# Last image's z loaded with channels outermost, its outputs in the tiles of y, and a cast moved from ScalarE to GpSimd

## Chip, cores and metric

The kernel runs on one core of one Trainium2 chip. The metric is the device time of one execution in microseconds (us); lower is better. The engines are named as in the profile: PE is TensorE (PEld its weight loads), DVE is VectorE, ACT is ScalarE, POOL is GpSimd and SP is SyncE, which here only issues DMAs.

## The reference, cut to what matters

The input x is 16 images of 56 x 56 pixels and 384 channels in f32. Two layers follow each other, each with a group normalisation over 32 groups of 12 channels and a residual addition.

```python
# layer 0: dilated attention; three groups of channels with dilations 1, 2, 3; 12 heads of 32 channels
qkv = einsum('bchw,oc->bohw', groupnorm(x), w_qkv)
attn = softmax(einsum('bgdn,bgdkn->bgnk', q, unfold3x3(k, dil)) * 32 ** -0.5)
y = einsum('bgnk,bgdkn->bgnd', attn, unfold3x3(v, dil))
x = x + einsum('bhwc,oc->bhwo', y, w_proj) + b_proj
# layer 1: depthwise 3x3 convolution with weights binarised to their sign
x = x + depthwise3x3(groupnorm(x), sign(w))
```

## The kernel before

An image is cut into 7 chunks of 8 rows, that is 448 pixels; there are 112 chunks. A chunk passes three plans. `plan_a` loads x, turns it so that channels lie on partitions and writes it to a scratch tensor `xd` in DRAM, taking statistics. `plan_b` is the attention: project q, k and v, score the nine neighbours, softmax, weigh v, project the output, add the residual and write the result to a scratch tensor `x1d` in DRAM, taking statistics again. `plan_c` is the convolution: it loads `x1d` back, normalises it, applies the taps, adds the residual, turns the result back to pixels on partitions and writes the output.

Each piece of work of a plan is registered with `at(when, order, piece)`: a step number, with 9 steps per chunk, and a class that orders the pieces within a step. The classes are listed once, SOFTMAX first, then SCORE, STATISTICS, CONVOLVE, WEIGH, QUERY, SPREAD, QKV, PROJECT and so on, LOADS last. The pieces are then emitted in sorted order. A tile framework turns them into one instruction queue per engine, in which instructions run strictly in order, and inserts the waits; it may move instructions of one queue against each other when it builds the program. DMAs from SP and ACT share eight completion semaphores in turn.

The softmax of a chunk ends in the f32 tile `ew`. TensorE spreads the weights over channels in bf16, so `ew` is split into three bf16 terms in the tile `e3`: `softmax_3` casts `ew` to the first term on ACT (L558) and subtracts it on POOL, giving `rest` (L559); `softmax_4` casts `rest` to the second term on ACT (L563) and subtracts that on POOL, giving the third term (L564). `turn_weights` sends `e3` through a DMA transpose into `aT` (L569). `weigh` then multiplies: TensorE spreads into `pb_a` (L582), DVE multiplies with v into a tile `w` (L589, three such buffers), POOL adds up the products (L597, L600, L601) into the tiles `y` (pool `y_p`, four buffers of 128 x 448), and `out_project` uses them (`po`, L615).

In `plan_c`, two of the three blocks of 128 channels (j = 0, 1) are convolved on TensorE. A tile `z` holds 32 channels (one of four sets q) on three times 32 partitions, one third for each row shift ky, so that one matmul sums over the three rows. The third block goes through nine multiply-adds: on ACT and POOL for images 0 to 14 (L768, L774), on DVE for the last image (`taps_last`, L759), whose loads and work nothing else overlaps any more. For the last image `z` lives in buffers that the attention has left: four of pool `t_p` for even chunks; three of `w_p` and the one of `xr_p` for odd chunks; each holds two sets q. So the loads of chunk c+2 wait until chunk c has been convolved. `normalise` scales them in place (L703 on ACT, L699 on DVE for q = 3), `convolve` runs 24 matmul instructions for each j (`pc`, L717) and DVE adds the residual (L724). `turn` transposes the result (`pt_o`, L789), copies it out of PSUM on ACT to `osb` (L791; pool `o_p`, two buffers) and stores it (L794), on SP for images 0 to 14, on ACT for the last.

The loads of `z` have two forms. Images 0 to 14, and the first and last chunk of the last image, use one DMA per row shift ky (L684), with 32 channels outermost. The five middle chunks of the last image use one DMA per set q (L692), which reads the three shifted rows as the outermost dimension of its source:

```python
one = by_set[:, q, p0 - W : p0 - W + PX]
three_rows = bass.AP(one.tensor, one.offset, [(W, 3), *one.ap])
nc.sync.dma_start(set_of(j, q), three_rows)
```

The functions that the diff touches, and what calls them:

Of the kernel before, what the change touches and what calls it, by code (L numbers as in the profile page):

```python
# [8 lines left out]
F32 = mybir.dt.float32  # L9
# [8 lines left out]
P = 128  # L18
# [4 lines left out]
NQ = 4  # L23
ROWS = 8
SUB = 112
# [10 lines left out]
def dilated_attention_then_binary_conv(  # L36
# [28 lines left out]
    nc = tc.nc  # L65
    B, H, W, C = x.shape
    PX = ROWS * W
    NCH = H // ROWS
# [82 lines left out]
    y_p = ctx.enter_context(tc.tile_pool(name="y_p", bufs=4))  # L151
# [5 lines left out]
    o_p = ctx.enter_context(tc.tile_pool(name="o_p", bufs=2))  # L157
# [234 lines left out]
    def at(when, order, piece):  # L392

        pieces.setdefault((when, order), []).append(piece)
# [50 lines left out]
    def plan_b(m, t0):  # L445

        b, c = divmod(m, NCH)
# [104 lines left out]
        e8 = ew.rearrange(EIGHTS, k=8)  # L552
        term = [e3.rearrange("p s u (r k) -> p (s u r) k", r=4)[:, :, 8 * t : 8 * t + 8] for t in range(TERMS)]

        def softmax_3():

            had["rest"] = rest = s_p.tile([SUB, NSUB * NPAD * HEADS], F32, tag="rest", name="rest")
            nc.scalar.copy(term[0], e8)  # L558
            nc.gpsimd.tensor_tensor(rest.rearrange(EIGHTS, k=8), e8, term[0], ALU.subtract)  # L559

        def softmax_4():
            r8 = had["rest"].rearrange(EIGHTS, k=8)
            nc.scalar.copy(term[1], r8)  # L563
            nc.gpsimd.tensor_tensor(term[2], r8, term[1], ALU.subtract)  # L564

        def turn_weights():
# [67 lines left out]
        at(t0 + 9, SOFTMAX, softmax_1)  # L634
        at(t0 + 10, SOFTMAX, softmax_2)
        at(t0 + 11, SOFTMAX, softmax_3)
        at(t0 + 12, SOFTMAX, softmax_4)
        at(t0 + 12, LOADS, turn_weights)
        for i in range(9):
            at(t0 + 14 + i, WEIGH, lambda i=i: weigh(i))  # L640
# [4 lines left out]
    def plan_c(m, t0):  # L645

        b, c = divmod(m, NCH)
        p0 = c * PX
        had = {}

        def edges(j):
            found = []
            for z, _, _ in had[f"z{j}"]:
                if c == 0:
                    found.append(z[0:HD, :, 0:W])
                if c == NCH - 1:
                    found.append(z[2 * HD : 3 * HD, :, PX - W : PX])
            return found

        def set_of(j, q):  # L660
            return next(z[:, q - q0] for z, q0, q1 in had[f"z{j}"] if q0 <= q < q1)

        def load(j):
            by_set = x1d[b].rearrange("(j q c) n -> j c q n", q=NQ, c=HD)[j]
            if b < B - 1:
                z = z_p.tile([P, NQ * PX], F32, tag="z", name="z")[:K3].rearrange("p (q n) -> p q n", q=NQ)
                had[f"z{j}"] = [(z, 0, NQ)]
            else:

                had[f"z{j}"] = []  # L670
                for q0 in range(0, NQ, 2):
                    pool, tag = (t_p, "t") if c % 2 == 0 else (w_p, "w") if (j, q0) != (1, 2) else (xr_p, "xr")
                    z = pool.tile([P, 3, PX], F32, tag=tag, name="z_last")[:K3, :2]
                    had[f"z{j}"].append((z, q0, q0 + 2))
            for edge in edges(j):
                nc.gpsimd.memset(edge, 0.0)
            for ky in range(3):
                lo = W if c == 0 and ky == 0 else 0
                hi = PX - W if c == NCH - 1 and ky == 2 else PX
                n0 = p0 + (ky - 1) * W  # L680
                for z, q0, q1 in had[f"z{j}"]:
                    if b == B - 1 and 0 < c < NCH - 1:
                        continue
                    nc.sync.dma_start(  # L684
                        z[ky * HD : (ky + 1) * HD, :, lo:hi], by_set[:, q0:q1, n0 + lo : n0 + hi]
                    )
            if b == B - 1 and 0 < c < NCH - 1:

                for q in range(NQ):
                    one = by_set[:, q, p0 - W : p0 - W + PX]  # L690
                    three_rows = bass.AP(one.tensor, one.offset, [(W, 3), *one.ap])
                    nc.sync.dma_start(set_of(j, q), three_rows)  # L692

        def normalise(j):
            mrz = mr1[b][1]
# [88 lines left out]
        def turn(s):  # L784
            pt = ps_mt.tile([P, 512], F32, tag="mt", name="pt_o")
            mid = had["xg"][:, 1 : ROWS + 1, :].rearrange("p r w -> p (r w)")
            for j in range(NG):
                src = mid if j == JG else had["x1"][:, j]
                nc.tensor.transpose(pt[:SUB, j * P : (j + 1) * P], src[:, s * SUB : (s + 1) * SUB], ident)  # L789
            osb = o_p.tile([SUB, C], F32, tag="osb", name="osb")  # L790
            nc.scalar.copy(osb, pt[:SUB, :C])  # L791

            queue = nc.sync if b < B - 1 else nc.scalar
            queue.dma_start(of[b, p0 + s * SUB : p0 + (s + 1) * SUB, :], osb)  # L794

        if b == B - 1:

            at(t0 - 12, LOADS, load_g)
            at(t0 - 3, LOADS, load_x)
            ahead = 8 if c else 1  # L800
            at(t0 - ahead, NORM, normalise_g)
            for j in range(JG):
                at(t0 - 12 + j, LOADS, lambda j=j: load(j))
                at(t0 - ahead + j, NORM, lambda j=j: normalise(j))
                at(t0 + 1 + j, CONVOLVE, lambda j=j: convolve(j))
            for ky in range(3):
                at(t0 + 1 + ky, CONVOLVE, lambda ky=ky: taps_last(ky))
            for s in range(NSUB):
                at(t0 + 12, STAGE_C, lambda s=s: turn(s))
            return  # L810
# [9 lines left out]
        for j in range(JG):  # L820
            at(t0 - 4 + 3 * j, LOADS, lambda j=j: load(j))
            at(t0 - 1 + 3 * j + late, NORM, lambda j=j: normalise(j))
            at(t0 + 2 + 3 * j + late, CONVOLVE, lambda j=j: convolve(j))
        for s in range(NSUB):
            at(t0 + 9 + s, STAGE_C, lambda s=s: turn(s))

    SOFTMAX, SCORE, STATISTICS, CONVOLVE, WEIGH, QUERY, SPREAD, QKV, PROJECT, STAGE_A, STAGE_C, NORM, LOADS = range(13)
# [43 lines left out]
    for m in range(N):  # L871
        plan_a(m, start_a(m))
        plan_b(m, STEP * m)
        plan_c(m, STEP * (m + 10))
# [31 lines left out]
```

## Time and profile before

| what | value |
|---|---|
| time, median of 3 runs | 5360.88 us (5352.83 to 5364.77) |
| the profiled execution, its own time | 5362.08 us |
| its span in the profile | 5360.3 us |
| mean granted TensorE clock | 0.981 |
| busy share of PE, PEld, DVE, ACT, POOL | 97%, 44%, 78%, 45%, 78% |
| first convolution of the last image on PE | 5229.86 us |
| last convolution of the last image ends | 5346.75 us |

The page gives busy time, share of the span and number of instructions of each engine, then the span in 40 slices, in which a digit is a tenth. A row of a group reads: line, engine, operation, tiles and shapes, count | busy us in all, mean ns of one | idle time of the engine just before these instructions, and what ended it. In a timeline a row is start, length, engine, line, operation and count, with the idle time ahead of it in brackets. SPq and ACTq are the sequencers that issue DMAs: the length of such a row is the issue, not the transfer.

### The profile page before, as it was taken

The numbers are of one execution on the slowest core, as the hardware profiler recorded it, in microseconds if no ns is written. First come the engines' busy times: TensorE is split into PE (matmuls) and PEld (weight loads), VectorE is DVE, ScalarE is ACT, GpSimd is POOL, SyncE is SP. The second block draws the span as 40 slices with busy tenths as digits, with TensorE's granted clock in tenths as the row PEclk, the third lists the DMA queues.
The fourth block names the chain that finished last, engine by engine and source line by source line (L and its number), as shares of the span: only waits on it lengthen the run. The fifth ranks groups of instructions, "written<-read, shape, count | busy, mean of one in ns | idle before, by whom it ended". The sixth has DMA issues, their size and how long they took to land.

```text
span 5360.3 us, 76299 instructions
## 1 busy us (share of the span) xinstructions
PE 5174.7 (97%) x27333; PEld 2385.0 (44%) x27333; DVE 4189.1 (78%) x4125; ACT 2400.3 (45%) x4189; POOL 4178.0 (78%) x2839
## 2 busy tenths in 40 slices
PE   8999999999999999999999999999999999999965
PEld 4444444444444444444444444444444444444422
DVE  4887887877888788888888888887788878777754
ACT  3223444444444544444444444544444444444433
POOL 2677888878888888888888888887888888788880
PEclk8999999999999999999999999999999999999976
DMA  6444556655656555555665556655555655444443
GB/s 194 124 116 116 160 163 165 165 153 161 166 157 169 159 163 154 163 155 160 165 165 160 158 160 166 166 157 162 162 154 160 165 157 162 134 129 135 123 130 128
DMA packets 810793, 825.66 MB, mean 154 GB/s; under 512 B 359467, under 2 KB 800174, under 8 KB 810414
## 3 DMA queue, kind: packets, MB, share of 16 engines
q1 hardware_dynamic: 802430, 808.79, 54.9%
q10 hardware_dynamic: 7984, 12.00, 0.7%
q8 instruction: 216, 3.54, 0.3%
q14 instruction: 163, 1.34, 0.1%
HBM read 466.41 MB, written 231.21 MB: 130 GB/s over the span
## 4 chain that ended last, share of the span: by engine, by line
PE 77%; POOL 7%; DVE 7%; DMA 4%; ACT 2%; issue 1%; SPq 1%; POOLq 0%; ACTq 0%; DVEq 0%
PE pkv L463 23%; PE pq L463 13%; PE po L615 11%; PE ps L501 10%; PE pc L717 8%; PE pb_a L582 5%; POOL w L597 3%; DVE t L516 3%; DVE w L589 2%; PE pt_x L422 2%; PE pt_o L789 2%; POOL m L774 2%; PE pt_s L536 1%; ACT m L768 1%; DMA z_last<-x1d 1%
## 5 line engine op out<-in xcount | busy, mean ns | idle before, releaser
L597 POOL TENSOR_TENSOR w<-w 128x1344 f32<-128x1344 f32 x672 | 2051.6, 3053 | 420.6 <-DVE w L589 376.1
L589 DVE TENSOR_TENSOR w<-pb_a,v 128x1344 f32<-128x1344 f32 x1008 | 1558.9, 1547 | 266.6 <-PE pb_a L582 176.7
L516 DVE TENSOR_TENSOR t<-pq,k 128x1344 f32<-128x1344 f32 x1008 | 1536.1, 1550 | 228.9 <-PE pq L463 228.0
L463 PE MATMUL pkv<-xn,wqkvT 128*128 128x448 f32 x3924 | 1569.6, 549 | 11.7 <-ACT osb L791 5.7
L463 PEld LDWEIGHTS pkv<-xn,wqkvT 128*128 128x128 f32 x3924 | 718.4, 190 | 683.2 <-issue 637.5
L774 POOL TENSOR_TENSOR m<-m 128x1344 f32<-128x1344 f32 x210 | 644.5, 3069 | 281.7 <-ACT m L768 281.5
L615 PE MATMUL po<-y,wprojT 128*128 128x448 f32 x2016 | 834.7, 550 | 18.3 <-POOL y L601 14.7
L463 PE MATMUL pq<-xn,wqkvT 128*128 128x448 f32 x1962 | 830.7, 557 | 0.0
L703 ACT ACTIVATE z<-z,mrz 96x448 f32<-96x448 f32 x840 | 578.2, 751 | 360.9 <-DMA z<-x1d 325.3
L501 PE MATMUL ps<-t,sel 128*32 128x448 f32 x6048 | 663.4, 548 | 28.7 <-DVE t L516 28.0
L768 ACT ACTIVATE m<-zg,ktap 128x448 f32<-128x448 f32 x945 | 555.5, 658 | 274.2 <-POOL m L774 267.2
L615 PEld LDWEIGHTS po<-y,wprojT 128*128 128x128 f32 x2016 | 376.6, 192 | 375.8 <-issue 344.0
L717 PE MATMUL pc<-z,kdiag 96*32 96x440 f32 (+1 forms) x5040 | 517.6, 544 | 5.7 <-POOL z L705 4.6
L463 PEld LDWEIGHTS pq<-xn,wqkvT 128*128 128x128 f32 x1962 | 343.9, 189 | 316.9 <-issue 316.9
L601 POOL TENSOR_TENSOR y<-y,w 128x448 f32<-128x448 f32 x336 | 382.0, 1137 | 23.7
L582 PE MATMUL pb_a<-aT,spread 24*128 24x448 bf16 x3024 | 368.6, 359 | 32.5 <-DVE w L589 27.3
L600 POOL TENSOR_TENSOR y<-w 128x448 f32<-128x448 f32 x336 | 382.8, 1139 | 14.5
L618 DVE SCALAR_TENSOR_TENSOR xr<-po,bias,xr 128x448 f32<-128x448 f32 x336 | 227.5, 677 | 202.7 <-PE po L615 197.7
L724 DVE TENSOR_TENSOR x<-pc,x 128x448 f32<-128x448 f32 x224 | 139.1, 621 | 307.3 <-PE pc L717 295.0
L473 ACT COPY v<-pkv 128x448 f32<-128x448 f32 x336 | 178.6, 531 | 448.1 <-PE pkv L463 429.9
L473 ACT COPY k<-pkv 128x448 f32<-128x448 f32 x336 | 178.8, 532 | 401.5 <-PE pkv L463 401.4
L501 PEld LDWEIGHTS ps<-t,sel 128*32 128x32 f32 x6048 | 170.2, 109 | 365.7 <-issue 237.5
(131 smaller groups left out, 4324.0 us busy)
## 6 DMA issues: line engine op xcount, KB each, us to landing
z<-x1d SPq DMA_DIRECT2D x570, 224.0 KB
xr<-xd SPq DMA_DIRECT2D x112, 672.0 KB
x1d<-xr SPq DMA_DIRECT2D x112, 672.0 KB
xn<-xd SPq DMA_DIRECT2D x109, 672.0 KB
xin<-in_x_dram SPq DMA_DIRECT2D x105, 672.0 KB
xd<-xa SPq DMA_DIRECT2D x315, 224.0 KB
out_dram<-osb SPq DMA_DIRECT2D x420, 168.0 KB
x<-x1d SPq DMA_DIRECT2D x112, 448.0 KB
```

The source lines that it names most:

```text
L463: nc.tensor.matmul(dst[:, :PX], wqkvT[:, cc, o0 : o0 + P], had["xn"][:, cc, :], start=(cc == 0), stop=(cc == NG - 1))
L501: return nc.tensor.matmul(had["ps"][32 * j : 32 * j + 32, :PX], sel[:, s0 : s0 + 32], tk, start=(issued[j] == 1), stop=(issued[j] == len(r ...
L516: nc.vector.tensor_tensor(t.rearrange("p k (r w) -> p k r w", w=W), q3, k3, ALU.mult)
L582: return nc.tensor.matmul(pb[:, kx, :PX].rearrange("p (s n) -> p s n", s=NSUB), spread[rows_of, v % 2, :], had["a"][rows_of, :, v // 8, :] ...
L589: nc.vector.tensor_tensor(w.rearrange("p k (r w) -> p k r w", w=W), pb[:, :, :PX].rearrange("p k (r w) -> p k r w", w=W), three(kv[1][g][m ...
L597: nc.gpsimd.tensor_tensor(w0, w0, w, ALU.add)
L600: nc.gpsimd.tensor_tensor(y, w0[:, 0], w0[:, 1], ALU.add)
L615: nc.tensor.matmul(po[:, :PX], wprojT[:, g, j * P : (j + 1) * P], had[f"y{g}"], start=(g == 0), stop=(g == NG - 1))
L703: nc.scalar.activation(z, z, AF.Identity, bias=mrz[:, j, q, 0:1], scale=mrz[:, j, q, 1:2])
L717: return nc.tensor.matmul(pcr[q * HD : (q + 1) * HD, :, lo:hi], kdiag[:, kx, j * NQ + q, :], rows(set_of(j, q))[:, :, lo + kx - 1 : hi + k ...
L768: nc.scalar.activation(rows(t[:, kx]), zp[:, ky : ky + ROWS, kx : kx + W], AF.Copy, scale=ktap[:, o : o + 1])
L774: nc.gpsimd.tensor_tensor(had["m"], had["m"], t, ALU.add)
```

## The change

The second term of the split is cast on POOL instead of ACT, and the subtraction that gives `rest` is registered as a piece of its own with a later class in the same step. The five middle chunks of the last image load `z` in the form of all other chunks: three row shifts times two tiles for each j, 12 DMAs of 32 channels x 2 sets x 448 in place of 8 DMAs of 96 x 448 per chunk, 60 in place of 40 in all. The output tiles of the last image come from the four buffers of `y_p` instead of the two of `o_p`.

```diff
         def softmax_3():
-            had["rest"] = rest = s_p.tile([SUB, NSUB * NPAD * HEADS], F32, tag="rest", name="rest")
             nc.scalar.copy(term[0], e8)
+
+        def softmax_4():
+            had["rest"] = rest = s_p.tile([SUB, NSUB * NPAD * HEADS], F32, tag="rest", name="rest")
             nc.gpsimd.tensor_tensor(rest.rearrange(EIGHTS, k=8), e8, term[0], ALU.subtract)
 
-        def softmax_4():
+        def softmax_5():
             r8 = had["rest"].rearrange(EIGHTS, k=8)
-            nc.scalar.copy(term[1], r8)
+            nc.gpsimd.tensor_copy(term[1], r8)
             nc.gpsimd.tensor_tensor(term[2], r8, term[1], ALU.subtract)
...
         at(t0 + 11, SOFTMAX, softmax_3)
-        at(t0 + 12, SOFTMAX, softmax_4)
+        at(t0 + 11, PROJECT, softmax_4)
+        at(t0 + 12, SOFTMAX, softmax_5)
...
                 for z, q0, q1 in had[f"z{j}"]:
-                    if b == B - 1 and 0 < c < NCH - 1:
-                        continue
                     nc.sync.dma_start(
                         z[ky * HD : (ky + 1) * HD, :, lo:hi], by_set[:, q0:q1, n0 + lo : n0 + hi]
                     )
-            if b == B - 1 and 0 < c < NCH - 1:
-
-                for q in range(NQ):
-                    one = by_set[:, q, p0 - W : p0 - W + PX]
-                    three_rows = bass.AP(one.tensor, one.offset, [(W, 3), *one.ap])
-                    nc.sync.dma_start(set_of(j, q), three_rows)
...
-            osb = o_p.tile([SUB, C], F32, tag="osb", name="osb")
+            if b < B - 1:
+                osb = o_p.tile([SUB, C], F32, tag="osb", name="osb")
+            else:
+                osb = y_p.tile([P, PX], F32, tag="y", name="osb_last")[:SUB, :C]
             nc.scalar.copy(osb, pt[:SUB, :C])
```

In the program that results, the queue of GpSimd is the same but for the inserted copy, which stands right behind `rest` or, in some chunks, one instruction later.

More of the change, by code (lines that the diff above doesn't have):

```diff
@@ L555, in softmax_3 @@
         def softmax_3():
+            nc.scalar.copy(term[0], e8)
+        def softmax_4():
             had["rest"] = rest = s_p.tile([SUB, NSUB * NPAD * HEADS], F32, tag="rest", name="rest")
-            nc.scalar.copy(term[0], e8)
             nc.gpsimd.tensor_tensor(rest.rearrange(EIGHTS, k=8), e8, term[0], ALU.subtract)
-        def softmax_4():
+        def softmax_5():
             r8 = had["rest"].rearrange(EIGHTS, k=8)
-            nc.scalar.copy(term[1], r8)
+            nc.gpsimd.tensor_copy(term[1], r8)
             nc.gpsimd.tensor_tensor(term[2], r8, term[1], ALU.subtract)
```

## The prediction

> **What bounds the kernel now.** I read the first lines of the page, then the slices, then the waits of TensorE, then the end of the span in order of time.
>
> ```profile
> span 5360.3 us, 76299 instructions
> PE 5174.7 (97%) x27333; PEld 2385.0 (44%) x27333; DVE 4189.1 (78%) x4125; ACT 2400.3 (45%) x4189; POOL 4178.0 (78%) x2839
> PE   8999999999999999999999999999999999999965
> PEclk8999999999999999999999999999999999999976
> ```
>
> TensorE is busy 97%. The slices show where the missing 3% lies: the body is full, and the last two slices (134 us each) fall to 6 and 5, with the granted clock down to 7 and 6. So the span has two parts with different limits. In the body, from 500 to 5050 us, gaps of TensorE sum to only about 50 us: work moved between other engines gains almost nothing there, and costs only if it makes TensorE wait. The tail is the convolution of the last image. TensorE's timeline there gives the start of each of its seven chunks; these are the first groups of five of them:
>
> ```profile
> 5244.57 5.91 PE L717 MATMUL pc<-z_last,kdiag 96*32 96x448 f32 x48
> 5282.24 4.66 PE L717 MATMUL pc<-z_last,kdiag 96*32 96x448 f32 x24
> 5304.57 4.40 PE L717 MATMUL pc<-z_last,kdiag 96*32 96x448 f32 x24
> 5328.60 6.56 PE L717 MATMUL pc<-z_last,kdiag 96*32 96x448 f32 x48 [0.97 <-ACT osb L791]
> 5338.57 4.23 PE L717 MATMUL pc<-z_last,kdiag 96*32 96x448 f32 x24 [1.79 <-POOL z_last L705]
> ```
>
> With the starts at 5229.86 and 5259.36 the six steps between chunks are 14.7, 14.8, 22.9, 22.3, 24.0 and 10.0 us, together 108.7. The SyncE timeline of the slow steps shows what fills them:
>
> ```profile
> 5287.90 21.08 SPq L692 DMA_DIRECT2D z_last<-x1d  x9
> 5309.09 2.08 SPq L709 DMA_DIRECT2D x<-x1d  x1
> 5311.27 0.39 SPq L735 DMA_DIRECT2D xg_last<-x1d  x1
> 5328.96 7.70 SPq L684 DMA_DIRECT2D z_last<-x1d  x8
> ```
>
> SyncE is held by the loads of z in the form of L692: about 2.2 us for one. The loads of the last chunk use L684 and go out in under a us each, and the step that they feed is the short one. The windows of a slow step and of the short one (columns: length, busy us of PE, PEld, DVE, ACT, POOL, then clock, DMA share, GB/s) show the DMA engines themselves:
>
> ```profile
> 5282.20:5304.60 22.40, 12.62 (x65) 4.08 (x65) 7.98 (x13) 6.89 (x11) 0.00 (x0) 0.50 0.38 127
> 5328.60:5338.60 10.00, 8.21 (x61) 3.11 (x62) 9.36 (x16) 4.57 (x8) 0.40 (x2) 0.81 0.79 246
> ```
>
> A slow step keeps 0.38 of the 16 DMA engines busy, no compute engine is full, and yet everyone waits for data. In the 40 slices of 5260 to 5310 us the quiet ones move 75 to 77 GB/s at one to two tenths: three engines of 16 are 0.19. One L692 load is 32 channels x 3 rows x 1,792 B = 172 KB; at 76 GB/s that is 2.26 us, the time that one issue takes. Forty of them are 90 us, and they run from 5216 to 5319. **The tail is bound by three DMA engines.**
>
> **What the Trainium skill says.** "DMA: Bandwidth & Descriptors", section "Why a DMA increments its semaphore by 16 and not by 1": a DMA runs on the largest number of engines up to 16 that divides the slowest dimension of both sides. With 3 rows outermost at the source and 96 partitions at the destination that is 3; with 32 outermost on both sides it is 16. The trace agrees (75 to 77 GB/s beside two tenths). "GPSIMD Engine Reference", section "4.1 Engine selection": one-input work on GpSimd is roughly line-rate, two-input about 2x slower than VectorE. The trace has no one-input copy on GpSimd; its 112x512 memset took 514 ns, its two-input 112x512 subtraction 1,160 ns. "TensorE: Matmul & The Clock Gate", Part 1: the clock halves when TensorE is idle and recovers after about 3.4 us of sustained work. Here 24 matmuls of pc took 4.66 us in the slow steps and 2.44 us at 5234.52.
>
> **The change part by part.**
>
> *Loads of z.* The 40 L692 loads go; 60 of 32 channels x 2 sets x 448 (115 KB, the same bytes) come. The nearest row is L684's own 24 loads of z_last: issue 0.42 us in the median. Twelve per chunk are 5.0 us of SyncE, plus about 0.4 each for x and xg: 5.8. Each chunk moves 1.38 MB of z, 0.46 of x, 0.29 of xg and 0.69 of output, 2.8 MB; at the 246 GB/s of the short step 11.4 us at most, and at the 355 GB/s of the best slice 7.9. Loads of chunk c+2 wait for the convolution of c, a step and more ahead, so they leave the path. What is late next is a loop between ScalarE and TensorE. The changed program's order has, per chunk: six normalisations and one of xg, TensorE's two convolutions, its transposes of the chunk before, four osb copies with their DMA issues, then the next normalisations. The path is three normalisations (3 x 0.755 = 2.3), both convolutions (5.9, as at 5244), a first transpose (0.5), four copies and issues (4 x (0.48 + 0.32) = 3.2): 11.9 us. ScalarE's sum per chunk is 4.5 + 0.85 + 3.2 = 8.6, VectorE's 2 x 0.51 + 2 x 0.62 + 9 x 0.68 = 8.4: both fit. I take 10 us for the first step, whose loads begin at 5215.8 and so, at 12 x 0.42 us and some 4 us for outputs between and the landing, are there by 5226, and 12 for the other five: 70 us for 108.7, **-39 us**. Bounds: 10.0 for all (the short step) gives -49; with both convolutions at half clock (9.3) a step is 15.3 and the sum 86.5, -22. The first convolution at 5229.86 does not move: it waits for the statistics.
>
> *Outputs in tiles of y.* After the last convolution ends at 5346.75, eight osb copies run from 5347.26 to 5356.8; with two buffers, every other one waits 0.5 to 1.8 us for an output DMA. With four buffers and copies back to back: 8 x 0.8 = 6.4 us for 9.5, **-3 us**. The y tiles are free by then.
>
> *The cast.* Per chunk ScalarE loses L563 (618 ns) and the wait ahead of it (229.3 us in 112 = 2.05 us); GpSimd gains one copy behind its own subtraction. Nothing else changes places on GpSimd or TensorE in the body; ScalarE takes sT one place earlier once per image, and SyncE swaps neighbours here and there, the weights' transpose with a halo copy of half a us or so among them.
>
> ```profile
> L559 POOL TENSOR_TENSOR rest<-ew,e 112x512 f32<-112x512 f32 x112 | 130.0, 1160 | 167.0 <-ACT e L558 167.0
> L564 POOL TENSOR_TENSOR e<-rest,e 112x512 bf16<-112x512 f32 x112 | 129.8, 1159 | 1.5 <-ACT e L563 1.5
> L563 ACT CAST e<-rest 112x512 bf16<-112x512 f32 x112 | 69.2, 618 | 229.3 <-POOL rest L559 229.3
> ```
>
> Before, GpSimd filled that time with a 3 us addition (L597) and waited for the cast 1.5 us in all, so the new copy is pure added length: I take 0.6 us (between 0.51, the memset, and 1.16, the subtraction), 67 us of GpSimd in all. Queued behind it are L597 and the second subtraction, whose w tiles VectorE waits for, and behind VectorE TensorE. The cover is GpSimd's idle time: after rest it takes 7 to 12 us in most chunks (18 at image ends) to have idled 0.6 us, and TensorE is not waiting meanwhile. The transpose of the weights has 2.5 to 10.4 us (median 8.0) from the end of its issue to its first use; where it has 2.5 (1 or 2 chunks) it was already the wait. Where GpSimd runs without pause, at the end of each image (pb_a waits 0.6 us for DVE w, which waited for GpSimd: 809, 1129, 1451 us and so on), I let the copy through in full: 14 x 0.6 = +8. The stretch 5094 to 5160 is GpSimd's too: two casts there, of which one stood in the chain on ScalarE before, +0.6. On the other side ScalarE stood 6.87 us at L563 at 4652 and held TensorE for 2.83 us through osb; the same gap stands at 4970: -5.7. Together **+3 us**. Bounds: twice the price and no relief +20; a gain of a few us more, since ScalarE frees transpose results earlier, -8.
>
> *Sum.* -39 - 3 + 3 = -39 us. The profiled execution took 5362.08 us for a span of 5360.3, 1.2 over the median 5360.88: 5362.1 - 39 = 5323, against the median **5322 us**.
>
> **The rivals.** (1) *Slower: GpSimd becomes the bound.* If the copy costs 1.16 us and reaches TensorE in every chunk, 112 x 1.16 = +130, less 42 from the tail: 5449. It decides from 42 / 112 = 0.38 us per chunk on. For it: 78% busy, over 80% in steady stretches, and the queue is in order. Against it: the idle time above and TensorE's 50 us of gaps in 4,550. (2) *The clock stays at half and the tail's loop gives back half:* -22 - 3 + 3 gives 5339. For it: 0.50 to 0.57 in the slow steps; against it: 0.81 in the short one. (3) *The new loads do not spread or cost per load:* 60 x 1.5 us = 90 us and the tail stands, 5362. Against it: L684's loads are of this very shape. (4) *The tail runs at its floor:* steps of 10, 5312 or a little below.
>
> **How the numbers follow.** Forecast (steps of 11 to 13) 0.55, half clock 0.18, floor 0.15, no spread 0.06, GpSimd bound 0.06. A measurement of this kernel can tell 0.2%, 11 us, from no change. The first three are all faster by more than that: 0.88; same 0.06; slower 0.06. The range 5303 to 5346 takes in the floor with some gain in the body and the half clock with a dearer cast; the last two lie outside.
>
> **What would show it.** Right: no L692 form; SyncE's z_last issues near 0.42 us; chunk starts in the tail 10 to 13 us apart; no wait of osb for output DMAs at the end; the cast on GpSimd near 0.6 us and TensorE's gaps in 500 to 5050 within 10 us of 50. Wrong: steps still over 18 us, or waits of pb_a and po for GpSimd in every chunk.

## The result, and the profile after

The changed kernel takes **5365.67 us** (median of 20 executions) beside 5360.24 us of the kernel before: a ratio of 1.0012 with a 95% interval of 1.0005 to 1.0018. By the bound of the prediction, 0.2%, this is no difference, though the interval leaves out 1: if anything the change is 5 us slower. Faster by 39 us had been forecast. A ratio below always comes with its interval and is against the kernel before, run on the same chip.

First the top of the page of the changed kernel and two of its slice rows:

```profile
span 5364.1 us, 76279 instructions
PE 5185.5 (97%) x27333; PEld 2395.0 (45%) x27333; DVE 4229.5 (79%) x4125; ACT 2326.1 (43%) x4077; POOL 4240.2 (79%) x2951
PE   8999999999999999999999999999999999999977
PEclk9999999999999999999999999999999999999987
```

The last two digits of PE went from 6 and 5 to 7 and 7, and the clock's from 7 and 6 to 8 and 7. So the tail did get better. TensorE's timeline gives its steps (start, length, and in brackets the idle time ahead):

```profile
5269.48 4.75 PE L712 MATMUL pc<-z_last,kdiag 96*32 96x448 f32 x24 [2.21 <-POOL z_last L700]
5280.04 2.53 PE L712 MATMUL pc<-z_last,kdiag 96*32 96x448 f32 x24
5292.61 8.06 PE L712 MATMUL pc<-z_last,kdiag 96*32 96x448 f32 x48 [4.86 <-DVE z_last L694]
...
5320.18 7.93 PE L712 MATMUL pc<-z_last,kdiag 96*32 96x448 f32 x48 [3.79 <-ACT z_last L698]
...
5347.24 8.04 PE L712 MATMUL pc<-z_last,kdiag 96*32 96x448 f32 x48 [3.72 <-POOL z_last L700]
```

With the starts at 5307.15 and 5333.53 the steps are 10.6, 12.6, 14.5, 13.0, 13.4 and 13.7, together 77.8 us in place of 108.7. From the first convolution to the end of the span it is 94.6 us, before 130.4: **35.8 us gained in the tail**, 30.9 of them in the steps and 4.7 behind the last convolution. But the first convolution starts at 5269.48 instead of 5229.86: **39.6 us lost in the body**. The question is where those come from.

The cast itself is as expected. Its row among GpSimd's groups:

```profile
L565 POOL CAST e<-rest 112x512 bf16<-112x512 f32 x112 | 68.2, 609 | 5.5
```

For 11 images of the body (800 to 4300 us) I compare the changed kernel with the one that has the tail's edits alone (first experiment), since the edits to their bodies differ by the cast only. The waits of ScalarE and VectorE there (columns: us in all, times, longest), first of the tail alone, then of the changed kernel:

```profile
ACT z L695 <- DMA z<-x1d: 248.0, 89, 4.3
...
DVE w L589 <- POOL w L597: 37.6, 36, 2.5
```

```profile
ACT z L698 <- DMA z<-x1d: 320.6, 82, 6.0
...
DVE w L591 <- POOL w L599: 96.9, 73, 4.2
```

VectorE waits twice as often for GpSimd's sums. That alone reads like "GpSimd is too slow now", and I took it so at first. The other row is the clue: ScalarE waits 73 us longer for DMA loads of z. It has less to do and may only come to the same wait sooner; but in e5 below, where its work is that of the tail alone, this wait is as long (322.9 us).

### The profile page after: what moved, and what is told of

Same layout as the page of the kernel before. It is cut to its first block, busy times and chain, and to the rows that moved or that the text cites. A ratio compares the mean times of both kernels' runs of the same rounds, so it can differ in the third digit from the quotient of the medians.

```text
span 5364.1 us, 76279 instructions
## 1 busy us (share of the span) xinstructions
PE 5185.5 (97%) x27333; PEld 2395.0 (45%) x27333; DVE 4229.5 (79%) x4125; ACT 2326.1 (43%) x4077; POOL 4240.2 (79%) x2951
## 5 line engine op out<-in xcount | busy, mean ns | idle before, releaser
L603 POOL TENSOR_TENSOR y<-y,w 128x448 f32<-128x448 f32 x336 | 382.1, 1137 | 22.7
L602 POOL TENSOR_TENSOR y<-w 128x448 f32<-128x448 f32 x336 | 382.3, 1138 | 14.5
L434 ACT COPY xa<-pt_x 128x448 f32<-128x448 f32 x315 | 167.4, 534 | 490.6 <-PE pt_x L422 490.6
```

Of the source, the lines that this page charges most:

```text
L602: nc.gpsimd.tensor_tensor(y, w0[:, 0], w0[:, 1], ALU.add)
L603: nc.gpsimd.tensor_tensor(y, y, w0[:, 2], ALU.add)
```

## Experiments

All times in us.

| label | what | time | ratio (95%) |
|---|---|---|---|
| e1 | tail's edits alone | 5324.53 | 0.9932 (0.9916, 0.9949) |
| e2 | cast alone | 5412.07 | 1.0090 (1.0075, 1.0105) |
| e3 | new loads alone | 5323.01 | 0.9932 (0.9919, 0.9944) |
| e8 | change, softmax sums in PSUM | 5418.48 | 1.0108 (1.0093, 1.0123) |
| e9 | e1, softmax sums in PSUM | 5383.18 | 1.0037 (1.0023, 1.0050) |
| e5 | e1 + unread copy ahead of the third term | 5366.98 | 1.0012 (1.0005, 1.0018) |
| e6 | e1 + unread copy behind it | 5326.03 | 0.9934 (0.9919, 0.9949) |
| e7 | e1 + two copies ahead of it | 5392.18 | 1.0061 (1.0044, 1.0078) |
| e11 | e1 with one GpSimd sum less | 5293.10 | 0.9872 (0.9858, 0.9887) |
| e10 | change, cast behind the next sum | 5399.20 | 1.0077 (1.0064, 1.0089) |
| e12 | change, rest and cast behind it | 5517.00 | 1.0293 (1.0279, 1.0307) |
| e13 | e1, rest behind it | 5491.45 | 1.0248 (1.0232, 1.0263) |
| e14 | e1, loads of z (j = 0) and xg on ACT's queue | 5321.99 | 0.9935 (0.9920, 0.9950) |
| e15 | e14 + the copy of e5 | 5331.83 | 0.9953 (0.9938, 0.9968) |
| e16 | change, loads of z (j = 0) and xg on ACT's queue | 5337.28 | 0.9964 (0.9953, 0.9976) |
| e17 | e1 + two DMA issues behind the transpose | 5479.45 | 1.0232 (1.0215, 1.0249) |

The experiments ran on four chips: e1, e2, e8 and e9 on one; e5, e6, e7 and e11; e3, e10, e12 and e13; e14 to e17. The kernel before took 5356.7 to 5362.4 us there, so a difference between rows of two chips can be off by some 5 us.

### The halves apart

e1 takes the diff's loads and outputs and leaves the softmax as it was; e2 takes the softmax hunk alone; e3 the loads alone.

```diff
# e1: only these hunks of the change
-            if b == B - 1 and 0 < c < NCH - 1:
...
+                osb = y_p.tile([P, PX], F32, tag="y", name="osb_last")[:SUB, :C]
# e2: only this hunk
-            nc.scalar.copy(term[1], r8)
+            nc.gpsimd.tensor_copy(term[1], r8)
# e3: e1, and back to
+            osb = o_p.tile([SUB, C], F32, tag="osb", name="osb")
```

> New loads of z and outputs in the tiles of y, with the cast left on ScalarE. Theory A (the cast on GpSimd costs some 40 us in the body and the tail gains what it was forecast to gain): about 5325 us, ratio to before 0.993, TensorE's first convolution of the last image near 5230 us as before, the L549 multiply of VectorE at its mean of 913 ns. Theory B (the body's loss has another source, for instance the new order of the last image's loads and outputs): about 5365, as the changed kernel.

> The cast on GpSimd alone, loads and outputs as before. Theory A: 5361 + 40 = about 5400 us, ratio 1.007, the first convolution of the last image near 5269 us as in the changed kernel, L549 near 1.2 us. Theory B: within 5 us of before.

> New loads of z alone; cast on ScalarE, outputs of the last image from the two buffers of o_p. The forecast gives the loads 39 us and the outputs 3: about 5327 us. If the outputs' two buffers hold the shorter tail up in every chunk, it is 5335 or more.

The tail is worth 38 us, close to the forecast 42; the cast costs 50 us without the tail's edits and 41 with them (5365.7 less 5324.5). The 9 us between these two prices are about what the intervals leave open, so the tail and the cast are, as far as can be told, two separate parts that happen to cancel. What the outputs are worth cannot be read from these times: e1 and e3 have the same ratio, each with some 8 us to either side, and 3 us had been forecast.

### Is it the two engines' collision on one multiplication?

In the change the softmax multiplication of VectorE, which reads two SBUF tiles, got longer. Its row in the kernel before, in the changed kernel, and in e8, where the sums stand in PSUM:

```profile
L549 DVE TENSOR_TENSOR ew<-ew,sm 112x432 f32<-112x432 f32 x112 | 102.3, 913 | 0.4
```

```profile
L549 DVE TENSOR_TENSOR ew<-ew,sm 112x432 f32<-112x432 f32 x112 | 135.9, 1213 | 0.4
```

```profile
L550 DVE TENSOR_TENSOR ew<-ew,ps 112x432 f32<-112x432 f32 x112 | 65.3, 583 | 0.0
```

The sum, 33.6 us, looks much like the loss. The Trainium skill's "SBUF — State Buffer", section "SBUF: two separate sides", says that a VectorE operation with two SBUF inputs and a GpSimd operation that reads SBUF lock each other out for a whole instruction. The trace agrees: with one input in PSUM the multiplication takes 571 to 606 ns, with two in SBUF 580 ns to 2.7 us.

```diff
-            sm = s_p.tile([SUB, NSUB, GH], F32, tag="sm", name="sm")
+            sm = had.pop("sums")[:SUB, PX : PX + NSUB * GH].rearrange("p (s k) -> p s k", s=NSUB)
```

> The changed kernel with the softmax's sums (sm) in the spare columns of the scores' PSUM tile, so that the L549 multiply has one SBUF input in place of two. Theory C (the loss is a collision: with the copy, GpSimd runs beside L549, which then takes 1.3 us instead of 0.6): L549 about 0.6 us in every chunk and the time 5320 to 5330. Theory D (the loss is the length of GpSimd's queue: w tiles come free later, VectorE waits, then TensorE): L549 also short, but the time stays near 5355 to 5365, and the distance to the same kernel with the cast on ScalarE stays near 35 us.

> As the run before it (sums in PSUM, new loads, outputs in the tiles of y), but with the cast on ScalarE; program orders of these two are the same but for the cast. Theory C: the same time as with the cast on GpSimd, within 8 us. Theory D: about 35 us less than it. Either way about 5320 us, since TensorE bounds the body.

With the multiplication at 583 ns in both, the cast still costs 35.3 us (e8 less e9): it can cost that much without the collision. But the pair stands on a changed base. Both kernels came out 53 to 59 us slower than the ones they start from (neither theory had expected that; TensorE's order changed with the edit, and why that costs was not followed). And their 35.3 us fall almost all on one place per image (2.1 of 2.7 us), while the change loses at several.

The traces of e1 and of the change settle more. TensorE's 27,333 instructions are the same in the same order in both, so each can be compared with its twin. Over chunks 14 to 97 TensorE falls back by 46 us in steps of over 0.1 us, and makes good 15. Of the 46, some 35 us stand behind a stop of VectorE for GpSimd's sum `w`, with no longer multiplication in between; 1 us stands behind the longer multiplication. **The collision is real, and is not what TensorE waits for.** Whether the longer multiplication also costs by making the first cast later, which stands behind it, is not shown; in e14 to e16 below it is short again (743 to 767 ns), so they do not tell either.

### Length on GpSimd, or its place?

The unread copy has the length of the cast (610 ns) and leaves the cast on ScalarE. In e5 it stands right behind `rest` in most chunks. In e6 it copies the third term (bf16, so half the bytes read) and stands behind it, in most chunks with one more sum of 1.14 us (`y`) between. e7 has the copy of e5 twice. e11 leaves one column of taps out of the third block's convolution.

```diff
# e5; e7 has the second line twice
             nc.gpsimd.tensor_tensor(rest.rearrange(EIGHTS, k=8), e8, term[0], ALU.subtract)
+            nc.gpsimd.tensor_copy(dump.rearrange(EIGHTS, k=8), had["rest"].rearrange(EIGHTS, k=8))
# e6
             nc.gpsimd.tensor_tensor(term[2], r8, term[1], ALU.subtract)
+            nc.gpsimd.tensor_copy(dump.rearrange(EIGHTS, k=8), term[2])
# e11
-        for kx in (1, 2, 3):
+        for kx in (1, 3):
```

> New loads and outputs, the cast on ScalarE as before, and a copy on GpSimd right behind rest that nobody reads (same size and bf16 output as the cast). Theory D (the length of GpSimd's queue): the time of the changed kernel, about 5362 to 5366, some 40 us over the same kernel without the copy (5324.5). Theory E (the loss comes from ScalarE: its copies run at other times once it no longer waits for rest): near 5325.

> The same copy, but of the third term, so that it stands behind the second subtraction and, in most chunks, a 3 us addition of w later in GpSimd's queue. Theory D1 (any added length costs the same, wherever it stands): about 5362 to 5366. Theory D2 (the place counts: right behind rest it delays the addition that frees the w tile VectorE waits for): 5325 to 5345.

> Two copies that nobody reads behind rest, about 1.2 us per chunk. If GpSimd bounds the steady chunks once 0.25 us per chunk of slack is used up, the second copy costs its whole length, 112 x 0.61 = 68 us, and the time is about 5430. If cost goes in proportion to the first copy: 5324.5 + 2 x 40 = about 5405.

> New loads and outputs, the cast on ScalarE, and one of the two 128x448 sums of the GpSimd taps left out in each chunk of images 0 to 14: this leaves one column of taps out of the third block's convolution. GpSimd loses 1.14 us per chunk. If GpSimd is near the bound of the body already without the copy, the time falls by 10 us or more, to about 5310; if TensorE alone bounds it, it stays at 5320 to 5325.

e5 costs 42 us over e1 with the cast still on ScalarE: so it isn't what ScalarE lost or got. **A copy of the same length behind the third term costs 1.5 us.** Their groups on GpSimd, e5 then e6, have the same mean to the nanosecond:

```profile
L561 POOL CAST dump<-rest 112x512 bf16<-112x512 f32 x112 | 68.3, 610 | 5.5
```

```profile
L566 POOL COPY dump<-e 112x512 bf16<-112x512 bf16 x112 | 68.3, 610 | 0.9
```

So it is not the 68 us that GpSimd works more. Two copies in the place of e5 cost 68 us, less than either of the forecasts for e7. GpSimd's length does count elsewhere: one sum less per chunk (1.14 us, in the convolution's sums ahead of the attention's) gained 31 us. Between the places of e5 and e6 stand, on GpSimd, above all one addition of products (`w`, 3.05 us) and the third term itself. One of the two must not be late.

### The addition, or the third term?

```diff
# e10: the cast behind the next addition; e12: rest too; e13: e1 with rest alone
+            with behind_last_sum():
+                nc.gpsimd.tensor_copy(term[1], r8)
...
-            nc.gpsimd.tensor_tensor(w0, w0, w, ALU.add)
+            last_sum[0] = nc.gpsimd.tensor_tensor(w0, w0, w, ALU.add)
```

`behind_last_sum` orders the instruction behind the addition that was emitted last, so the addition goes first and is no longer delayed by the cast.

> The changed kernel with one edit: the cast on GpSimd is queued behind the next addition of w (L597 of before) and no longer ahead of it; TensorE's and VectorE's orders are the same as in the changed kernel. Theory D2 (the copy cost 40 us because it delays the addition that gives VectorE its next w tile): 5320 to 5328 us, as with the cast on ScalarE (5324.5), VectorE's wait for POOL w back near 40 us in 800 to 4300. Theory D1 (any added length counts): 5360 or more.

> As the run before it, and the first subtraction (rest) is queued behind that addition too, so that the addition starts 1.16 us earlier than in any kernel so far. Theory D2: 5295 to 5315 us, if what leaving out one sum gave (-31 us for 1.14 us) was place and not length; the weights' transpose comes about as late as in the changed kernel. If the transpose becomes the wait of pb_a: 5320 or more.

> The cast on ScalarE as before, new loads and outputs, and the first subtraction queued behind the addition of w. Theory D2: 5295 to 5315 us. Without the place mattering: 5324.

All three are slower than what they start from, by 34 to 167 us, where theory D2 had forecast gains: **freeing the addition makes it worse.** What they delay is the third term. From the traces, over chunks 14 to 97, I took the median time from the end of the first cast to the end of the third term, and the mean time per chunk:

| kernel | first cast to third term | time per chunk |
|---|---|---|
| e1, e6 | 5.36 | 45.73 |
| change, e5 | 6.03 | 46.12, 46.15 |
| e10 | 7.01 | 46.58 |
| e7 | 7.68 | 46.33 |
| e13 | 8.50 | 47.66 |
| e12 | 8.94 | 47.84 |

But for e7 the time per chunk rises with this delay (e7 against e10 stays unexplained). The 0.39 us of the change times 105 chunks are 41 us, all of the loss. Yet TensorE hardly waits for what the third term feeds: the transposed weights are there some us early, as forecast. Something else must hang on it.

### What hangs on the third term

The answer came from laying two traces over each other. VectorE's instructions are the same 4,125 in the same order in e1 and in the change, so each can be compared with its twin. For one chunk, rows of the timelines of e1: SyncE, ScalarE, GpSimd, VectorE.

```profile
1622.45 1.16 POOL L564 TENSOR_TENSOR e<-rest,e 112x512 bf16<-112x512 f32 x1
...
1623.64 1.55 SPq L569 DMA_TRANSPOSE aT<-e  x1
...
1628.54 0.59 SPq L682 DMA_DIRECT2D z<-x1d  x1
...
1632.59 2.72 ACT L695 ACTIVATE z<-z,mrz 96x448 f32<-96x448 f32 x4 [2.47 <-DMA z<-x1d]
...
1635.66 0.85 ACT L738 ACTIVATE zg<-xg,mr 128x560 f32<-128x560 f32 x1 [0.35 <-DMA xg<-x1d]
...
1640.11 3.03 POOL L766 TENSOR_TENSOR m<-m 128x1344 f32<-128x1344 f32 x1 [1.56 <-ACT m L760]
...
1652.76 3.05 POOL L597 TENSOR_TENSOR w<-w 128x1344 f32<-128x1344 f32 x1
...
1656.44 1.55 DVE L589 TENSOR_TENSOR w<-pb_a,v 128x1344 f32<-128x1344 f32 x1
```

And the twins in the changed kernel:

```profile
1636.77 1.16 POOL L566 TENSOR_TENSOR e<-rest,e 112x512 bf16<-112x512 f32 x1
...
1637.96 1.54 SPq L571 DMA_TRANSPOSE aT<-e  x1
...
1642.94 0.58 SPq L685 DMA_DIRECT2D z<-x1d  x1
...
1647.37 2.72 ACT L698 ACTIVATE z<-z,mrz 96x448 f32<-96x448 f32 x4 [4.01 <-DMA z<-x1d]
...
1650.60 0.85 ACT L741 ACTIVATE zg<-xg,mr 128x560 f32<-128x560 f32 x1 [0.51 <-DMA xg<-x1d]
...
1655.09 3.04 POOL L769 TENSOR_TENSOR m<-m 128x1344 f32<-128x1344 f32 x1 [1.55 <-ACT m L763]
...
1667.77 3.04 POOL L599 TENSOR_TENSOR w<-w 128x1344 f32<-128x1344 f32 x1
...
1670.84 1.56 DVE L591 TENSOR_TENSOR w<-pb_a,v 128x1344 f32<-128x1344 f32 x1 [1.08 <-POOL w L599]
```

VectorE and TensorE run 13.24 us behind e1 here: the multiplication `t` ahead of this stretch starts at 1622.70 and at 1635.94. Subtract that from each pair: the third term is late by 1.08, the transpose by 1.08, the last of the z loads behind it by 1.16, ScalarE's z by 1.54, zg by 1.70, GpSimd's m by 1.74, its w by 1.77, and then VectorE's w stops for 1.08 us and is 14.40 behind. (Of the 1.08 of the third term, 0.67 come between `rest` and it, where the cast stands; `rest` was 0.41 late already.) Part of VectorE's lateness is made good; TensorE's next scores wait for it, in e1 and in the change:

```profile
1660.86 1.71 PE L501 MATMUL ps<-t,sel 128*32 128x448 f32 x16
```

```profile
1674.76 1.71 PE L501 MATMUL ps<-t,sel 128*32 128x448 f32 x16 [0.59 <-DVE t L516]
```

From here TensorE is 13.90 behind: 0.66 us are lost in this chunk, more than the mean of 0.39. The multiplication of the collision starts only after this.

SyncE issues in the order of its queue. In these traces it stands at the transpose until the third term is written (in this chunk of e1 from 13.5 to 19.9 us after the start of the scores' copy `sT`), and the loads of z and xg stand behind it, although they need nothing of it. They feed the convolution of an earlier image on ScalarE and GpSimd, and GpSimd's next sum of the attention is queued behind that. In this chunk the third term thus decides when the next chunk's sums come: a loop through five queues, and 0.6 us in it counts. Where the copy of e6 stands, it is past the loop's exit to SyncE.

One thing more differs. In the change, e2 and e5, in 60 of the 84 chunks 14 to 97, the framework issues the second of the three loads of z behind the transpose two places later than in e1; e6 has e1's order. The third load and the load of xg keep their places, and in all of the 30 chunks where the three landings can be read in both e1 and the change, the third lands last. So the swap does not make the last issue later. But where it stands, that load lands another 0.4 us later than the third term's delay alone would give (mean of 18 chunks), and elsewhere it does not. The swap without the copy was not run.

This was theory F, still an argument from two traces. The next runs take the loop apart. They move half of the loads of z, those of the first block (j = 0), and the load of xg.

```diff
# e14 (from e1) and e16 (from the change)
-                    nc.sync.dma_start(
+                    (nc.scalar if b < B - 1 and j == 0 else nc.sync).dma_start(
                         z[ky * HD : (ky + 1) * HD, :, lo:hi], by_set[:, q0:q1, n0 + lo : n0 + hi]
...
-            nc.sync.dma_start(
+            (nc.scalar if b < B - 1 else nc.sync).dma_start(
                 xg[:, lo:hi, :].rearrange("p r w -> p (r w)"),
# e15: e14 and the added line of e5
# e17 (from e1), behind the transpose in turn_weights
+            for n in range(2):
+                nc.sync.dma_start(spare[n], term[2][:, 0, :])
```

> The new loads of the tail with the cast on ScalarE; in addition the first load of z of each chunk (three DMAs) and the load of xg of images 0 to 14 are issued on ScalarE's queue instead of SyncE's, where they stood behind the transpose of the weights. It is the base for the two kernels that follow. Theory F (what costs is that SyncE's queue stands at the transpose until GpSimd's third term is there, and the loads of z and xg behind it come as late): these loads start 1 to 2 us earlier than with the tail alone, 5290 to 5325 us against 5324.5. Theory G (the copy costs by what GpSimd or the weights' transpose themselves do later, the loads behind it do not matter): within 10 us of 5324.5.

> The kernel just above with one unread 112x512 copy on GpSimd right behind rest, the edit that cost 42 us when the loads stood on SyncE's queue. Each other engine's order is that of the kernel just above. Theory F: the third term and the transpose come 0.6 us later as they did then, but no load of z or xg waits behind them: 0 to 12 us above the kernel just above. Theory G: 35 to 45 us above it.

> The changed kernel with the first load of z and the load of xg on ScalarE's queue. Theory F: the 41 us that the cast on GpSimd cost are gone, within 12 us of the tail alone with these loads on ScalarE's queue, and at most 5335 us. Theory G: 35 to 45 us above that kernel, 5355 to 5370 us.

> The tail alone, cast on ScalarE, with two small DMAs (112 rows of 16 bytes to a scratch tensor nobody reads) issued on SyncE's queue right behind each transpose of the weights; nothing is added to GpSimd. Theory F: the loads of z and xg come about 0.9 us later, as with one to two copies on GpSimd: 5350 to 5390 us. Theory G: the third term and the transpose are on time, so 5318 to 5332 us.

**With the loads on another queue the copy costs 9.8 us (e15 less e14) in place of 42**, though the third term is late by the same 0.67 us: 5.36 to 6.03 in the medians. The orders of all other engines are those of e14, but for one swap on SyncE, so this is the cleanest pair of the study. What it leaves open: e14's orders differ from e1's on every compute engine, so the copy's two prices are taken on two schedules. The changed kernel with these loads moved, e16, is 28 us faster than the change (26 by the ratios), and is 15.3 us over e14; at most 12 and at most 5335 had been expected, so most of the loss goes this way and a part does not. e16's rows in the same window, where ScalarE waited 320.6 us for z in the change:

```profile
ACT z L698 <- DMA z<-x1d: 1.7, 4, 0.7
...
DVE w L591 <- POOL w L599: 45.6, 11, 4.2
```

ScalarE now issues these loads itself and waits elsewhere for them (95.3 us ahead of `xa`). The waits of VectorE fell from 73 to 11, one per image. In e14 they are 16.6 us and in e15 22.7, 11 each. So the remaining 10 to 15 us are at least in part the one place per image at which GpSimd runs without pause, the place that the prediction had priced (+8).

Theory G, by which lateness acts on GpSimd or through the transposed weights alone, had forecast 35 to 45 us over e14 for e15 and e16 and fits neither. (e14 alone fits both theories.)

e17 adds nothing to GpSimd, and its third term is on time (5.36 in the median), but it is 155 us slower than e1, where theory G had forecast no loss and theory F 26 to 66. It is no clean price. The two issues hold SyncE for 1.85 us behind the transpose (median; 0.9 had been expected, and e1 has 0.05 there). And the framework also put ScalarE's normalisation of z behind five of its taps, in many chunks. It shows that loads late on SyncE's queue go with a loss when the third term is not late. Its wait for the load of xg, 87.4 us in e1:

```profile
ACT zg L741 <- DMA xg<-x1d: 325.5, 56, 8.3
```

The kernel before and the changed one are both beaten by e1, e3 and e14, which agree within 3 us: the tail's new loads with the cast left on ScalarE. Moving the loads of z to ScalarE's queue pays only beside the cast; alone it is nothing (5321.99 against 5324.53). That would fit loads which in e1 come just in time, but this was not tested.

## Why the prediction was wrong

**What bounds the kernel: right in the tail.** The tail was bound by three DMA engines, and the new form removed that. That the body can lose was right too, but not taken seriously enough. That it has almost nothing to win was wrong: e11, with 1.14 us less on GpSimd per chunk, gained 31 us.

**Loads of z, -39: right in kind, measured -30.9** in the six steps. The term mis-sized is "both convolutions (5.9, as at 5244)" in the path of a step. They take 7.6 to 8.1 us in the last five chunks, with a mean clock of 0.59 to 0.62 while they run; in the second chunk, in a step with a clock of 0.99, they take 5.1. The window of one step of the changed kernel (length, busy us of PE, PEld, DVE, ACT, POOL, clock, DMA share, GB/s):

```profile
5320.20:5333.50 13.30, 9.54 (x60) 5.38 (x60) 8.23 (x13) 6.89 (x12) 0.74 (x4) 0.76 0.73 210
```

Over the whole step the clock is 0.76, up from 0.50; TensorE still idles 3.8 us of it for the normalisation. Steps of 13 to 14.5 in place of 12 are the difference; rival 2 (half clock) lay on the other side of it.

**Outputs, -3: right at its place.** From the end of the last convolution to the end of the span it is 8.8 us in the change and in e1, 13.6 in the kernel before and 13.0 in e3. The times of e1 and e3 do not show it, and need not: their traces start the first convolution of the last image at 5226.14 and 5219.93, though their orders in the body are the same. That is within the scatter from one execution to the next (e1's four lie between 5320.3 and 5329.4 us), which is larger than the term.

**Price of the copy, 0.6: right**, 609 ns.

**The cast's cost, +3 (bounds -8 to +20): wrong, measured +39.6; this is the step that failed.** Its words: "The cover is GpSimd's idle time: after rest it takes 7 to 12 us in most chunks (18 at image ends) to have idled 0.6 us, and TensorE is not waiting meanwhile." The idle time is there, but it covers only what leaves by GpSimd's own queue. e6 shows that it covers a copy nearly in full; the third term leaves by SyncE's queue 1.2 us after it starts, long before that idle time. The transpose had been looked at, with 2.5 to 10.4 us to its first use, and the slack was right for the weights. Of what stands behind the transpose on SyncE the prediction said only that SyncE "swaps neighbours here and there"; it did not ask who consumes the loads of z and xg there. The instruction that waits had slack; those queued behind it had none to spare. With them on another queue the same copy costs 9.8 us (e15), close to the +8 that the prediction had for the ends of the images. Its own sign showed the failure: TensorE's idle time from 500 to 5050 us, which was to stay within 10 us of 50, went from 45 to 69.

**ScalarE's relief, -5.7: given back.** The two gaps of 2.8 us at 4651 and 4970 are gone. The waits of TensorE from 4600 to 5060 us show what came in their place, in the changed kernel:

```profile
PE pb_a L584 <- DMA aT<-e: 6.5, 2, 3.3
```

In the kernel before this wait was 0.7 us. In this stretch the late transpose does reach TensorE directly.

**The rivals.** Rival 1 had the sign and not the way. It asked for 0.38 us per chunk through GpSimd's backlog to cancel the tail; the body lost 39.6 / 112 = 0.35 us per chunk, so the sum landed at no change by coincidence of two sizes, an outcome that had been given 0.06. Doubling the price of the copy bounded the wrong quantity: the unknown was not how long it takes but what it makes late.

## What to carry to other kernels

When an instruction that another queue waits for becomes later, list what stands behind the waiting instruction on that in-order queue and who consumes it, before calling the slack of the waiting one a cover. Here a loop through several queues showed as many small waits and no single bound; it was found by laying two traces with the same instruction order over each other and reading which instruction is late first. Two edits that pay in different stretches must be timed apart, as here a gain of 38 us stood hidden behind a loss of 41.

## What the runs showed of the hardware that was not expected

A VectorE multiplication of 112x432 with two inputs in SBUF has a mean of 913 ns in the kernel before and 1,213 in the changed one, without any change to it; with one input in PSUM it has a mean of 583 and never takes more than 606 (e8, e9). Moving that input to PSUM did not make the kernel faster. And 610 ns of GpSimd per chunk, 68 us of work in all, cost 42 us or 1.5 us (e5, e6) with the same length, above all one addition and the third term between the two places.
